# A channel norm in six parts: squares, roots and reciprocals each one part later

## The chip, the cores and the metric

The kernel runs on one core of a Trainium2 chip. The metric is the device time of one execution in microseconds. Before the change three runs took 6383.12, 6406.59 and 6412.63 us; their median is 6406.59 us. The profile is of one further execution.

The engines are named as in the profile: PE is TensorE, and PEld its weight loads; DVE is VectorE, ACT ScalarE, POOL GpSimd, and SP is the queue that issues most DMAs. "L996" is line 996 of the kernel.

## The reference, cut to what matters

Two layers run one after the other over x of shape (4, 96, 128, 128). Layer 0 is a state-space block: a projection to 192 channels, a depthwise convolution, four scans over the image in different directions, and their sum `ym`. Layer 1 is a convolution block with attention. What is touched here is the end of layer 0, a norm over the 192 channels of each pixel and the projection back to 96 channels:

```python
ym = (y0 + y1 + y2 + y3).reshape(B, D_INNER, H, W).astype(x.dtype)
yn = jnp.moveaxis(ym, 1, -1)
mu = yn.mean(-1, keepdims=True)
var = yn.var(-1, keepdims=True)
yn = (yn - mu) * jax.lax.rsqrt(var + 1e-05) * ln_w + ln_b
yn = jnp.moveaxis(yn, -1, 1)
return jnp.einsum('bdhw,cd->bchw', yn, out_w) + out_b[None, :, None, None]
...
x = x + _L0_conv_ref(_gn(x), ...)
```

The mean is taken out of the projection's weights ahead of time, so that each pixel needs only one factor, 1/sqrt(var + eps), after the projection. The variance is made as the mean of the squares minus the square of the mean.

## The kernel before, in words

The whole program is one stream of instructions for each engine, made by Python generators. A generator emits some instructions and then yields a number, the cost of what it emitted. `co_run(left, right, pace)` weaves two of them: after each yield of `left` it adds cost times pace to a debt, and as long as the debt is above zero it lets `right` emit and takes its cost off.

The four images go through the same stages. First all four are projected. The scan (`ssm_scan`) runs over pairs of images and goes on beside the rest: it works in steps of 1024 pixels for 128 channels, and each step is two halves, each with a cost of 2.6. A half-step has three operations of VectorE (`times_b` L837, `scan` L854, `times_c` L858), matmuls that spread rows into PSUM (L747), and one addition or multiplication of GpSimd. The first half also has two softplus of ScalarE (L676) and, in every other step, two exp (L809); its GpSimd operation is L833. The second half has the GpSimd addition L866, the store L875, and in every other step six loads of `xrows` on the SP queue (L735).

`ssm_output` is the norm. For image 0 it is `left` of a `co_run` with the scan at pace 0.65. For images 1 to 3 it is part of `right` (called `light`) beside the direct convolutions or the attention of the image before, at pace 1.0 or, for image 1's remainder beside the first attention, 1.5. The instructions up to the end of the scan are tied to the order of emission, engine by engine (`in_order`). After that the scheduler of the language gives each engine the instruction that is ready by its own reckoning, and among those the one emitted first.

The norm works in 16 chunks of 1024 pixels. Its loop has 18 turns. In turn c it does the first work on chunk c (`new`), the middle on chunk c-1 (`mid`), and the last on chunk c-2 (`old`). A turn has six parts, each ended by a yield:

1. the projection of `old` on PE (`projected`, L1023 and L1028), the squares and differences of `mid` (`inverse`, L996 to L998), the first squaring of `new` on ScalarE (`squares`, L959);
2. the root of `mid` on ScalarE (`roots`, L1002), the first half of `old` times its factor on VectorE (`scaled`, L1039 for image 0, L1037 for the others), the second squaring of `new`;
3. `back(mid)`: VectorE's reciprocal (L1006), GpSimd's issue of the write of `rd` (L1008), and SP's load of `xr` (L1010); then `added` for `old` on GpSimd (L1047 or L1045), the second half of `scaled`, and the first half of the means of `new` on PE (`sums`, L970);
4. the second half of `sums`, the second `added`, the statistics of the first half (`counted`, L1051), and the load of y for chunk c+1 (L951, L953);
5. `rows(new)`: ScalarE copies the means to `st` (L984 or L982) and issues four DMAs that reshape them into `mq` (L989); ScalarE adds a bias to `xr` (L1092); `spread_out(mid)` issues the read of `rd` into the tile `r` on GpSimd (L1016); the second `counted`;
6. the store of `old` (L1098).

The factor of a pixel thus passes through three DMAs: `mq` folds a row of 1024 means into 32 by 32, `rd` writes the factors to DRAM, and `r` reads them back to 96 partitions. Means of the values and of the squares lie in `mq`'s two planes.

The tiles `mq`, `xr` and `r` have two buffers each, `y` has three, `st` one. The PSUM pool of the norm has three banks in image 0 and two in the others; a chunk takes two for its projection and one for its sums.

Of the kernel before, what the change touches and what calls it, by code (L numbers as in the profile page):

```python
# [71 lines left out]
def kernel(  # L72
# [862 lines left out]
    def ssm_output(b, yms, xnew, stats, ps, side, turned):  # L935
# [5 lines left out]
        with tc.tile_pool(name="c2", bufs=2, side=side) as p2:  # L941
# [4 lines left out]
            def load_y(c):  # L946
                if c < NS:
                    y, rest = ys[c] = [
                        p2.tile([128, n], F32, name=m, bufs=3) for m, n in (("y", SN), ("yr", CH))
                    ]  # L950
                    nc.sync.dma_start(y, yms[0:128, bass.ts(c, SN)])  # L951
                    for h in range(2):
                        nc.sync.dma_start(  # L953
                            rest[64 * h : 64 * h + 64], yms[128:192, bass.ts(2 * c + h, CH)]
                        )

            def squares(c, j):
                sq = p2.tile([128, CH if j else SN], F32, name=f"sq{j}")
                nc.scalar.activation(sq, ys[c][j], AF.Square)  # L959
                sums_of[c, j] = sq  # L960

            def sums(c, j):
                sq = sums_of.pop((c, j))
                if j == 0:
                    sums_of[c] = bank(ps)
                pm = sums_of[c]
                for g in range(4):
                    rhs = sq if g % 2 else ys[c][j]
                    p = slice(64 * (g // 2), 64 * (g // 2) + 64) if j else slice(0, 128)
                    nc.tensor.matmul(  # L970
                        pm[32 * g : 32 * g + 32],
                        lhsT=mean192[p],
                        rhs=rhs[p, :] if j else rhs[:, bass.ts(g // 2, CH)],
                        start=(j == 0),
                        stop=(j == 1),
                    )
            def rows(c):
                st = p2.tile([128, CH], F32, name="st", bufs=1)
                pm = sums_of.pop(c)
                if turned:  # L980
                    to = st.rearrange("p (h j t) -> p h j t", j=TW, t=TN)
                    nc.scalar.copy(to, turned_view(pm))  # L982
                else:
                    nc.scalar.copy(st, pm)  # L984
                mq = made[c] = p2.tile([SN // TN, 2, TN], F32, name="mq")
                for i in range(2):
                    for h in range(2):
                        at = 32 * i + 64 * h
                        nc.scalar.dma_start(  # L989
                            mq[16 * h : 16 * h + 16, i],  # L990
                            st[at : at + 1].rearrange("p (a f) -> p a f", f=TN),
                        )

            def inverse(c):
                m, q = made[c][:, 0], made[c][:, 1]
                nc.vector.tensor_mul(m, m, m)  # L996
                nc.vector.tensor_sub(q, q, m)
                nc.vector.tensor_scalar(q, q, 0.0, None, ALU.max)  # L998

            def roots(c):  # L1000
                q = made[c][:, 1]
                nc.scalar.activation(q, q, AF.Sqrt, bias=eps[0 : SN // TN])  # L1002

            def back(c):
                q = made.pop(c)[:, 1]
                nc.vector.reciprocal(q, q)  # L1006
                to = rd[bass.ts(c, SN)]
                nc.gpsimd.dma_start(to.rearrange("(p f) -> p f", f=TN), q)  # L1008
                xr = p2.tile([C, SN], F32, name="xr")
                nc.sync.dma_start(xr, xb[:, bass.ts(c, SN)])  # L1010
                near[c] = xr, to

            def spread_out(c):
                xr, to = near[c]
                r = p2.tile([C, SN], F32, name="r")
                nc.gpsimd.dma_start(r, to.partition_broadcast(C))  # L1016
                near[c] = xr, r

            def projected(c):
                po = [part(ps, C, CH) for _ in range(2)]  # L1020
                y, rest = ys.pop(c)
                for h in range(2):
                    nc.tensor.matmul(  # L1023
                        po[h], lhsT=outws[:, 0], rhs=y[:, bass.ts(h, CH)], start=True, stop=False
                    )
                for h in range(2):
                    p = slice(64 * h, 64 * h + 64)
                    nc.tensor.matmul(  # L1028
                        po[h], lhsT=outws[p, 1], rhs=rest[p], start=False, stop=True
                    )  # L1030
                return po

            def scaled(c, h, po):
                r = near[c][1][:, bass.ts(h, CH)]
                if turned:
                    v = r.rearrange("p (h j t) -> p h j t", t=TN, j=TW)
                    nc.vector.tensor_mul(v, turned_view(po), v)  # L1037
                else:
                    nc.vector.tensor_mul(r, po, r)  # L1039

            def added(c, h):
                xr, r = (t[:, bass.ts(h, CH)] for t in near[c])
                if turned:
                    v = r.rearrange("p (h j t) -> p h j t", t=TN, j=TW)
                    nc.gpsimd.tensor_add(v, v, turned_view(xr))  # L1045
                else:
                    nc.gpsimd.tensor_add(xr, r, xr)  # L1047

            def counted(c, h):
                t = near[c][turned]  # L1050
                nc.vector.bn_stats(stats[:, 2 * c + h], t[:, bass.ts(h, CH)])  # L1051
# [4 lines left out]
            for c in range(NS + 2):  # L1056
                new, old = c < NS, c - 2 if c >= 2 else None
                mid = c - 1 if 1 <= c <= NS else None
                if old is not None:
                    po = projected(old)  # L1060
                if mid is not None:
                    inverse(mid)
                if new:
                    squares(c, 0)
                yield 1.2
                if mid is not None:
                    roots(mid)
                if old is not None:
                    scaled(old, 0, po[0])
                if new:  # L1070
                    squares(c, 1)
                yield 1.4
                if mid is not None:
                    back(mid)
                if old is not None:
                    added(old, 0)
                    scaled(old, 1, po[1])
                if new:
                    sums(c, 0)
                yield 1.4  # L1080
                if new:
                    sums(c, 1)
                if old is not None:
                    added(old, 1)
                    counted(old, 0)
                    load_y(c + 1)
                yield 1.4
                if new:
                    rows(c)
                if mid is not None:  # L1090
                    xr = near[mid][0]
                    nc.scalar.activation(xr, xr, AF.Identity, bias=outbs)  # L1092
                    spread_out(mid)
                if old is not None:
                    counted(old, 1)
                yield 1.4
                if old is not None:
                    nc.sync.dma_start(xnew[:, bass.ts(old, SN)], near.pop(old)[turned])  # L1098
                yield 1.4
# [1346 lines left out]
    class Image:  # L2446
# [26 lines left out]
        def norm(self, yms, ps, side):  # L2473
            yield from ssm_output(self.b, yms, self.xnew, self.stats, ps, side, self.b > 0)
# [223 lines left out]
```

## Time and profile before

| What | Value |
|---|---|
| median of three runs | 6406.59 us |
| the profiled execution's own time | 6409.68 us |
| its span, first to last instruction | 6407.8 us |
| mean granted TensorE clock | 0.902 |
| PE busy | 5253.4 us (82%) |
| DVE busy | 4699.9 us (73%) |
| ACT busy | 3759.4 us (59%) |
| POOL busy | 3238.6 us (51%) |
| norm of image 0 | 2096 to 2357 us |
| norms of images 1, 2, 3 | 3245 to 3527, 3955 to 4210, 4785 to 5035 us |

The busy shares are means over stages with different limits, so the norm has to be read from its own stretches. In a line of waits the numbers are the idle time in total, how often, and the longest. In a timeline the number in brackets is the engine's idle time before the instruction, and after the arrow stands what ended it. An instruction's duration can contain a wait inside the engine. DMA issues are not counted as busy.

### The profile page before, as it was taken

How to read it: one execution, taken by the hardware profiler on the slowest of the kernel's cores; microseconds unless marked ns; L12 is line 12 of the kernel's file. 1: busy time of each engine (PE TensorE's matmuls, PEld its weight loads, DVE VectorE, ACT ScalarE, POOL GpSimd, SP SyncE). 2: the span in 40 equal slices, each digit the busy share in tenths (PEclk: the TensorE clock that was granted, in tenths of full speed). 3: DMA queues.
4: the chain of work that ended last, by engine and by line, in shares of the span. 5: the costliest groups of instructions: out<-in, count | busy, mean ns of one | idle time of the engine just before them, and what ended most of it. 6: DMA issues, size and time to landing. Idle time of an engine off the chain costs nothing. (4 is left out here: it accounts for less than half of the span.)

```text
span 6407.8 us, 76468 instructions
## 1 busy us (share of the span) xinstructions
PE 5253.4 (82%) x23264; PEld 2254.8 (35%) x23264; DVE 4699.9 (73%) x7132; ACT 3759.4 (59%) x4770; POOL 3238.6 (51%) x2476
## 2 busy tenths in 40 slices
PE   6889988987888643989988588977888877889888
PEld 2333322322222111444433234345333444345553
DVE  4247878988989768989844686468774687988767
ACT  1247767787787666777622465466644665545642
POOL 1326757978879554979822234436304365022310
PEclk9899989998999765999999799989989888999989
DMA  6766777775675766676667686665776656967668
GB/s 155 175 160 189 198 199 199 214 221 163 198 202 171 202 183 207 196 213 179 182 185 195 166 228 163 195 169 156 214 199 184 175 149 165 245 167 180 191 168 221
DMA packets 897706, 1205.30 MB, mean 188 GB/s; under 512 B 230644, under 2 KB 745642, under 8 KB 884816
## 3 DMA queue, kind: packets, MB, share of 16 engines
q1 hardware_dynamic: 866640, 1145.36, 65.5%
q0 software_dynamic: 16336, 38.51, 2.3%
q10 hardware_dynamic: 14320, 16.54, 0.9%
q8 instruction: 187, 3.06, 0.2%
q14 instruction: 223, 1.83, 0.1%
HBM read 777.82 MB, written 345.62 MB: 175 GB/s over the span
## 5 line engine op out<-in xcount | busy, mean ns | idle before, releaser
L633 PE MATMUL bank<-y,wp 128*128 128x512 f32 (+3 forms) x3584 | 1310.9, 622 | 83.8 <-DMA y<-y 41.0
L866 POOL TENSOR_TENSOR y<-y,dl 128x1024 f32<-128x1024 f32 x384 | 1058.5, 2757 | 263.0 <-DVE dl L858 240.3
L833 POOL TENSOR_TENSOR dl<-dl,u 128x1024 f32<-128x1024 f32 x384 | 1008.8, 2627 | 253.1 <-ACT dA L809 121.1
L854 DVE TENSOR_TENSOR_SCAN dA<-dA,pBC 128x512 f32<-128x512 f32 x768 | 981.6, 1278 | 30.7
L2169 PE MATMUL bank<-y,wn 128*64 128x384 f32 (+5 forms) x2408 | 680.1, 507 | 58.3 <-DMA y<-x1d 34.1
L1477 PE MATMUL two<-ya,wd 128*64 128x192 f32 (+3 forms) x2376 | 582.2, 414 | 174.0 <-ACT odd L1550 65.1
L633 PEld LDWEIGHTS bank<-y,wp 128*128 128x128 f32 (+3 forms) x3584 | 456.2, 168 | 749.3 <-issue 651.1
L858 DVE TENSOR_TENSOR dl<-dA,pBC 128x512 f32<-128x512 f32 x768 | 528.5, 688 | 255.8 <-PE pBC L747 183.8
L747 PE MATMUL pBC<-xr,wbc 60*128 60x512 bf16 (+1 forms) x1536 | 457.8, 404 | 311.5 <-DVE dA L854 239.1
L1938 ACT COPY yb<-ya 64x768 f32<-64x768 f32 (+1 forms) x660 | 537.7, 815 | 195.5 <-PE two L1477 113.8
L676 ACT ACTIVATE dl<-pd,dtb 128x512 f32<-128x512 f32 x768 | 485.5, 684 | 187.9 <-PE pd L747 171.5
L1477 PE MATMUL two<-yb,wd 128*64 128x192 f32 (+3 forms) x2376 | 559.0, 400 | 4.0 <-ACT yb L1938 4.0
L837 DVE TENSOR_TENSOR pBC<-dl,pBC 128x512 f32<-128x512 f32 x768 | 527.5, 687 | 8.8 <-POOL dl L833 7.8
L2169 PEld LDWEIGHTS bank<-y,wn 128*64 128x64 f32 (+3 forms) x2408 | 310.3, 169 | 357.2 <-issue 186.2
L809 ACT ACTIVATE dA<-dl,negA 128x1024 f32<-128x1024 f32 x384 | 420.3, 1141 | 2.3
L1477 PEld LDWEIGHTS two<-ya,wd 128*64 128x64 f32 (+1 forms) x2376 | 262.2, 165 | 370.9 <-ACT odd L1550 75.0
L676 ACT ACT_TABLE_LOAD x248 | 318.2, 1283 | 91.9 <-PE pd L747 79.7
L747 PEld LDWEIGHTS <-wbc 60*128 60x128 bf16 (+1 forms) x1536 | 103.1, 96 | 752.1 <-issue 739.3
L1477 PEld LDWEIGHTS two<-yb,wd 128*64 128x64 f32 (+1 forms) x2376 | 289.7, 167 | 150.5 <-issue 42.1
L1477 PE MATMUL two<-ya,wa 128*96 128x384 f32 (+1 forms) x528 | 231.2, 521 | 72.9 <-DMA ya<-vp 27.0
L1550 ACT COPY odd<-two 128x384 f32<-128x384 f32 (+5 forms) x176 | 115.8, 658 | 291.3 <-PE two L1492 179.1
L1406 POOL TENSOR_TENSOR pl<-x 96x256 f32<-96x256 f32 (+3 forms) x396 | 275.2, 710 | 0.0
(322 smaller groups left out, 9105.4 us busy)
## 6 DMA issues: line engine op xcount, KB each, us to landing
u<-zb SPq DMA_DIRECT2D x192, 1024.0 KB
yms<-y SPq DMA_DIRECT2D x96, 512.0 KB
xn<-xnew SPq DMA_DIRECT2D x128, 384.0 KB
ya<-vp SPq DMA_DIRECT2D x120, 336.0 KB
y<-y SPq DMA_DIRECT2D x128, 258.2 KB
zb<-z SPq DMA_DIRECT2D x64, 512.0 KB
y<-yms SPq DMA_DIRECT2D x64, 512.0 KB
ya<-x1p SPq DMA_DIRECT2D x90, 336.0 KB
```

The lines of the kernel that those rows point to most:

```text
L633: nc.tensor.matmul(blocks(pz[p:e]), lhsT=ws[k][:, d, c : c + e - p], rhs=window(ys[k], at, d, n), start=(i == 0), stop=(i == len(terms) - 1),)
L676: nc.scalar.activation(dst, src, AF.Softplus, bias=bias)
L747: nc.tensor.matmul(p, lhsT=w[rows], rhs=xr[rows, at : at + CH], start=True, stop=True)
L809: nc.scalar.activation(live[m]["dA"], live[m]["dl"], AF.Exp, scale=negA[:, g % 3, k : k + 1])
L833: nc.gpsimd.tensor_mul(t, t, u_view(n))
L837: nc.vector.tensor_mul(p, live[n]["dl"][:, bass.ts(half, CH)], p)
L854: nc.vector.tensor_tensor_scan(h, h, p, init, ALU.mult, ALU.add)
L858: nc.vector.tensor_mul(live[n]["dl"][:, sl], live[n]["dA"][:, sl], live[n]["C", half])
L866: nc.gpsimd.tensor_add(v, v, t.rearrange("p (a b) -> p a b", b=W))
L1477: nc.tensor.matmul(of(to[p:e], r), lhsT=w[:, i, c : c + e - p], rhs=tiles(t[k][PAIR[i]][:, SLOT[i]], o, r), start=(k == 0), stop=False,)
L1938: nc.scalar.copy(yb[k][64 * h - 64 : 64 * h, :, :n], ya[k][0:64, :, h * TN : h * TN + n])
L2169: nc.tensor.matmul(pc[p:e, :n].rearrange("p (h w) -> p h w", w=W), lhsT=w[:, c : c + e - p], rhs=v[:, :, 0:W], start=(i == 0), stop=(i == ...
```

## The change

The three calls `inverse(mid)`, `roots(mid)` and `back(mid)` move from parts 1, 2 and 3 to parts 2, 3 and 4. Nothing else is changed. Inside their new part they come first, as they did in the old one: `inverse` stands ahead of `scaled(old, 0)`, `roots` ahead of `added` and `sums`, `back` ahead of the second half of `sums`. `rows`, which makes `mq`, stays in part 5, and so does `spread_out`, which reads `rd`. So there are three parts in place of two between `rows` and `inverse`, and one in place of two between `back` and `spread_out`.

```diff
@@ -1058,26 +1058,26 @@
                 mid = c - 1 if 1 <= c <= NS else None
                 if old is not None:
                     po = projected(old)
-                if mid is not None:
-                    inverse(mid)
                 if new:
                     squares(c, 0)
                 yield 1.2
                 if mid is not None:
-                    roots(mid)
+                    inverse(mid)
                 if old is not None:
                     scaled(old, 0, po[0])
                 if new:
                     squares(c, 1)
                 yield 1.4
                 if mid is not None:
-                    back(mid)
+                    roots(mid)
                 if old is not None:
                     added(old, 0)
                     scaled(old, 1, po[1])
                 if new:
                     sums(c, 0)
                 yield 1.4
+                if mid is not None:
+                    back(mid)
                 if new:
                     sums(c, 1)
                 if old is not None:
```

## The prediction

> **What bounds the kernel now.** I read the page for the span, then the busy table cut at the four norms, then the waits, over the whole run and by norm, then the timelines of single turns. Turn c is the pass of `ssm_output`'s loop with that c, in six parts; `mid` is chunk c-1, `old` is chunk c-2.
>
> The span, and the four norms (columns: stretch, its length, then busy us and instructions of PE, PEld, DVE, ACT, POOL, then granted clock, DMA share, GB/s):
>
> ```profile
> span 6407.8 us, 76468 instructions
> ...
> 2096.00:2357.00 261.00, 166.75 (x495) 34.01 (x493) 173.05 (x238) 163.97 (x187) 139.76 (x101) 0.76 0.71 208
> ...
> 3245.00:3527.00 282.00, 241.54 (x893) 88.37 (x894) 109.19 (x237) 77.83 (x124) 64.41 (x64) 0.92 0.68 186
> ...
> 3955.00:4210.00 255.00, 231.72 (x1307) 98.03 (x1307) 117.29 (x259) 119.66 (x168) 97.12 (x125) 0.98 0.65 179
> ...
> 4785.00:5035.00 250.00, 222.75 (x1239) 92.25 (x1237) 117.04 (x257) 115.16 (x162) 102.19 (x134) 0.97 0.66 186
> ```
>
> Two regimes. In image 0's norm, beside the scan, no engine passes 66%: it is a latency loop. In the other three PE is busy 86, 91 and 89%, DVE under 47%; there only PE's idle 40, 23 and 27 us can be won. The norms are 1048 of 6408 us; nothing else is touched.
>
> The waits, first of the whole run, then PE's in each of the four norms:
>
> ```profile
> POOL rd L1008 <- DVE mq L1006: 178.3, 37, 11.0
> DVE mq L996 <- DMA mq<-st: 177.3, 44, 8.6
> ...
> ACT mq L1002 <- DVE mq L998: 108.2, 39, 8.2
> ```
> ```profile
> PE bank L970 <- ACT sq L959: 54.2, 15, 7.5
> ...
> PE bank L970 <- DVE r L1037: 20.7, 6, 7.9
> ...
> PE bank L970 <- DVE r L1037: 9.8, 6, 3.7
> ...
> PE bank L970 <- DVE r L1037: 9.0, 5, 2.5
> ```
>
> VectorE, ScalarE and GpSimd stand idle on the chain that the diff moves, but PE, the bound of images 1 to 3, waits for `scaled` (L1037), which frees a PSUM bank. That stays in part 2.
>
> ScalarE in one turn of image 0 (turn 6; start, length, instruction, idle before it):
>
> ```profile
> 2176.61 2.43 ACTq L989 DMA_DIRECT2D mq<-st  x4
> 2179.09 1.15 ACT L1092 ACTIVATE xr<-xr,outbs 96x1024 f32<-96x1024 f32 x1 [2.51 <-issue]
> 2180.14 1.04 ACT L959 ACTIVATE sq<-y 128x1024 f32<-128x1024 f32 x1
> 2181.20 1.28 ACT L676 ACT_TABLE_LOAD   x1
> 2182.50 1.26 ACT L676 ACTIVATE dl<-pd,dtb 128x512 f32<-128x512 f32 x2
> 2183.78 1.28 ACT L1002 ACT_TABLE_LOAD   x1
> 2185.07 0.32 ACT L1002 ACTIVATE mq<-mq,eps 32x32 f32<-32x32 f32 x1
> 2185.30 0.61 ACT L959 ACTIVATE sq<-yr 128x512 f32<-128x512 f32 x1
> 2187.95 0.58 ACT L984 COPY st<-bank 128x512 f32<-128x512 f32 x1 [2.03 <-PE bank L970]
> ```
>
> With the four issues counted, ScalarE is full except for 2.03 us between `sq<-yr` and the copy, in which PE makes the sums of that square. The root and its table load sit in front of that square.
>
> VectorE in turns 6 and 13, the parts that matter:
>
> ```profile
> 2179.99 0.18 DVE L996 TENSOR_TENSOR mq<-mq 32x32 f32<-32x32 f32 x1
> 2180.47 2.60 DVE L997 TENSOR_TENSOR mq<-mq 32x32 f32<-32x32 f32 x1 [0.30 <-DMA mq<-st]
> ...
> 2293.33 0.34 DVE L1006 RECIPROCAL mq<-mq 32x32 f32<-32x32 f32 x1 [5.52 <-ACT mq L1002]
> ```
>
> A 32x32 subtraction that takes 0.18 us elsewhere takes 2.60 while GpSimd multiplies (L833, 2180.64 to 2183.02), and a reciprocal holds VectorE for 5.52 us until the root is done.
>
> **What the Trainium skill says.** "SBUF — State Buffer", Who interferes with whom: a VectorE instruction with two SBUF inputs and a GpSimd instruction that reads SBUF exclude each other, and the later one blocks fully. The 0.18 against 2.60 us agrees. "ScalarE: Activation LUTs", What ACT_TABLE_LOAD costs: 1283 ns for every change of set; the trace has a mean of 1283 ns. "DMA: Bandwidth & Descriptors", Anatomy of one DMA: about 2 us fixed, mostly the receipt of the last write. The trace is longer, 4.2 us median to landing for `mq<-st` and 4.4 for `rd<-mq`, and those durations are used.
>
> **The change part by part.** Nothing is added or removed. Per chunk three small VectorE operations (0.18+0.18+0.17 us), one root (0.32, with a 1.28 us load), one reciprocal (0.34), the GpSimd issue of `rd` (0.54) and SP's load of `xr` move. What counts is what they are moved past.
>
> *Image 0* is held to the order of emission. The norm's parts cost 1.2 and 1.4, times the pace 0.65: 0.78 and 0.91; a half-step of the scan costs 2.6. So two half-steps fall in a turn (A with softplus, B without): after parts 2 and 5 in turns 1 to 4, after 1 and 4 in turns 5 to 10, after 6 and 3 in turns 11 to 16. The engines' order in the trace agrees. Only in turns 5 to 10 do the squares cross any scan work; elsewhere they stay between the same VectorE instructions.
>
> Turns 5 to 10 (turn 6 by hand). A starts at 2180.0 and not 2183.2, ends 2182.8; the squares follow, free of the GpSimd multiply at 2183.0, done 2183.7. On ScalarE `sq<-yr` comes at 2183.8 and not 2185.3, and the root (1.28+0.32) falls into the 2.03 us in which the copy waits. ScalarE's loop shrinks by 1.6. But `scaled` cannot start before r lands, and that loop grows: `scaled` to reciprocal now has both halves ahead of it (0.69+0.66=1.35 for 0.65), then 0.7 to the issue of rd, 6.4 to its landing (mean of these six), 0.4, 4.9 for r: 13.9 us, where it was 13.2. The pitch was 14.7 (2166.1 to 2239.8, five turns), so 0.8 a turn is left: 6 x 0.8 = -5 us. GpSimd then stands some 1.3 us longer before the r issue, since only one addition and L866 lie between; what is queued behind it is L833 of the next step, which VectorE needs a half-step later: hidden.
>
> Turns 11 to 16 (turns 12 and 13). The reciprocal moves behind B (2.75 us), the rd issue behind L866 (2.35): in turn 12 rd goes at 2280.5 for 2277.2, r lands 3 us later (2290 for 2287.0). In turn 13 the reciprocal no longer blocks B, which starts at 2291.3 for 2294.1; r lands 2 us earlier there (2301.4 for 2303.4). Over a pair that is no loss, and ScalarE's 1.6 can come through: the copy waited 1.2 to 3.6 us here too. On SP the `xr` load falls behind six `xrows` loads (5.46 us) in three turns; ScalarE's L1092 waits for it, I take 1 us each. 6 x -1.6 + 3 = -7 us.
>
> Turns 1 to 4. The root moves behind softplus and exp of A. In turn 1 that makes rd 4.5 us later and r's landing 2.8 after the old start of `scaled`; after that 0.7 a turn (the second half of `scaled` ahead of the reciprocal), partly returned because `sq<-yr` no longer waits for the squares (3.9 us in turn 3). +4 us.
>
> Image 0: -5 -7 +4 = -8 us.
>
> *Images 1 to 3* are ordered by the scheduler, near the order of emission. Counting there in the kernel before, other VectorE work lies between parts 1 and 2 in only 9 of 48 turns; in the other 39 the squares wait at the same place, and the 162 us of waits in these three windows stay. ScalarE gets one to three attention operations and `sq<-yr` ahead of the root in most turns: its waits for the squares (49.9+24.1+30.1) shrink, but ScalarE is busy under half of the time and PE waits little for it. Against this the rd issue may fall behind `added` (1.53 us), in the dozen of 45 turns where only its rank put it in front. r arrives last before `scaled` in 21 of 48 turns, so a dozen times 1.5 us half passed on is some +5; the 9 crossings and freed ScalarE some -5. I take 0; the bounds are -22 and +24 (rivals).
>
> Sum: -8 us. Against the profiled execution (6409.7 us, 1.9 outside its span) 6401.7; against the median of the runs, 6406.6, it is 6399.
>
> **Rivals.** *Faster.* ScalarE's loop sets image 0 alone: 12 turns x -1.6 = -19, the roots' waits in turns 2 to 4 another -5; and in images 1 to 3 half of PE's 45 us of waits for `scaled` (39.5 above and 5.8 at L1023 in image 1) go, -22. 6360 us. For it: 21 `scaled` start right behind squares that waited for mq. Against it: the squares still stand ahead of `scaled`, and r's landing follows `scaled` with 0.1 to 1.9 us of slack.
>
> *Slower.* One mechanism: r lands later, because reciprocal and rd go one part later while the r issue stays. It decides where the slip passes r's slack, 0.9 us on the mean for the chunks of turns 5 to 10. Image 0: turn 12's 3 us in all six late turns and not in every other, +18, and +4 early; images 1 to 3: 21 turns with r last x 1.5 us, three quarters reaching PE, +24. 6452 us. For it: L1016 already waits 46.2 us for rd in 18 turns, with two parts of room. Against it: in 22 of 45 turns the scheduler put the reciprocal ahead of `scaled` by readiness, where rank doesn't matter.
>
> *It does nothing* in three quarters of the turns, and the order elsewhere settles to the same pitch: 6407.
>
> **How the numbers follow.** No two runs tell a difference under about 0.5% (32 us). Likeliest with its near neighbour "nothing": 0.46, own range 6378 to 6432, almost all inside 0.5%. Faster rival 0.28, slower 0.26, each mostly beyond 0.5%. Hence 0.28, 0.46, 0.26. The range reaches to both rivals, with 1 in 10 outside on each side: 6348 to 6456.
>
> **What would show it.** Right: in image 0 the copy L984's wait for PE falls from 25.4 us to a few, the reciprocal's 21.9 us wait for the root goes, L1016's wait for rd and L1039's for r (7.8) grow; image 0's norm ends some 8 us earlier. In images 1 to 3 the wait L996 for mq stays near 160 us and PE's idle time within 10 us. Wrong, if L996's wait falls by half and PE's waits for L1037 with it (faster), or L1037's wait for r rises beyond 80 us (slower), or if the scheduler lays images 1 to 3 out anew.

## The result, and the profile after

The changed kernel takes 6419.09 us in the median of 22 runs (6403.12 to 6436.19), the kernel before 6405.17 in 22 runs beside them (6383.12 to 6414.72). The ratio is 1.0023, with a 95% interval of 1.0014 to 1.0032: 15 us slower, 9 to 20. When it was run again later beside others the ratio was 1.0017 (1.0007 to 1.0026). The forecast was 6399, so a small gain was expected and a small loss came; it lies inside the range, and inside the half per cent that the prediction called no change.

The span and the four norms of the kernel after (columns as before: stretch, length, busy us and instructions of PE, PEld, DVE, ACT, POOL, granted clock, DMA share, GB/s):

```profile
span 6415.1 us, 76484 instructions
...
2100.00:2359.00 259.00, 161.26 (x496) 33.01 (x493) 170.18 (x237) 163.47 (x187) 139.74 (x100) 0.76 0.73 209
3236.00:3534.00 298.00, 251.19 (x917) 91.80 (x915) 117.46 (x250) 79.69 (x128) 66.66 (x64) 0.91 0.65 181
3942.00:4205.00 263.00, 238.37 (x1340) 102.97 (x1340) 118.99 (x262) 125.26 (x175) 103.12 (x135) 0.98 0.65 183
4775.00:5039.00 264.00, 236.29 (x1252) 95.53 (x1248) 119.34 (x263) 116.34 (x164) 102.19 (x135) 0.95 0.63 179
```

Here each stretch runs from the first load of y to the last statistics of the image. With these borders the four norms of the profiled kernel before took 260.3, 289.6, 263.5 and 250.8 us; those of the kernel after 258.9, 298.1, 263.0 and 263.6. In image 3's norm PE does the same 1252 matmuls, but is busy for 236 us, where the kernel before needed 227 in the same borders, at a clock of 0.95 where it had 0.97. The kernel before, there:

```profile
4781.00:5032.00 251.00, 226.62 (x1252) 94.34 (x1248) 117.89 (x263) 116.82 (x164) 102.20 (x135) 0.97 0.67 189
```

The waits of the whole run that the prediction had shown, in the kernel after:

```profile
DVE mq L996 <- DMA mq<-st: 179.6, 44, 8.3
...
POOL rd L1008 <- DVE mq L1006: 137.1, 37, 9.7
ACT mq L1002 <- DVE mq L998: 135.3, 40, 9.2
```

VectorE's wait for the folded means (177.3 before) has hardly moved. PE's largest wait by total in each of the four norms, in order:

```profile
PE bank L970 <- ACT sq L959: 39.1, 13, 7.2
...
PE bank L970 <- DVE r L1037: 23.7, 5, 9.7
...
PE two L1477 <- ACT odd L1550: 7.6, 3, 3.4
...
PE bank L970 <- DVE r L1037: 12.2, 5, 4.5
```

In image 0, PE waits less for the square: 39.1 us for 54.2. In images 1 and 3 it waits 3 us more for `scaled`, in image 2 3 us less (6.8 for 9.8).

ScalarE in turn 6 of image 0, kernel after:

```profile
2183.44 1.15 ACT L1092 ACTIVATE xr<-xr,outbs 96x1024 f32<-96x1024 f32 x1 [2.57 <-DMA mq<-st]
2184.49 1.04 ACT L959 ACTIVATE sq<-y 128x1024 f32<-128x1024 f32 x1
2185.55 1.28 ACT L676 ACT_TABLE_LOAD   x1
2186.85 1.26 ACT L676 ACTIVATE dl<-pd,dtb 128x512 f32<-128x512 f32 x2
2188.00 0.63 ACT L959 ACTIVATE sq<-yr 128x512 f32<-128x512 f32 x1
2188.65 1.28 ACT L1002 ACT_TABLE_LOAD   x1
2189.94 0.32 ACT L1002 ACTIVATE mq<-mq,eps 32x32 f32<-32x32 f32 x1
2190.17 0.56 ACT L984 COPY st<-bank 128x512 f32<-128x512 f32 x1
```

This is what the prediction drew by hand: the square `sq<-yr` now stands ahead of the root and its table load, and the copy L984 follows the root without a wait (2.03 us before). What took its place stands in VectorE's waits in image 0's norm:

```profile
DVE r L1039 <- DMA r<-rd: 25.0, 13, 3.9
DVE xstats L1051 <- POOL xr L1047: 14.6, 11, 1.6
DVE mq L1006 <- ACT mq L1002: 13.7, 4, 5.7
```

`scaled` (L1039) now waits for r, the factors on their way back to 96 partitions, 13 times and 25.0 us, where it waited 4 times and 7.8 us; the reciprocal's wait for the root fell from 21.9 to 13.7.

### The profile page after: what moved, and what is told of

It is laid out like the page before. It is cut to its first block, busy times and chain, and to the rows that moved or that the text cites. A ratio compares the mean times of both kernels' runs of the same rounds, so it can differ in the third digit from the quotient of the medians.

```text
span 6415.1 us, 76484 instructions
## 1 busy us (share of the span) xinstructions
PE 5258.1 (82%) x23264; PEld 2259.2 (35%) x23264; DVE 4702.3 (73%) x7132; ACT 3759.1 (59%) x4770; POOL 3241.7 (51%) x2476
## 5 line engine op out<-in xcount | busy, mean ns | idle before, releaser
L866 POOL TENSOR_TENSOR y<-y,dl 128x1024 f32<-128x1024 f32 x384 | 1059.3, 2759 | 268.6 <-DVE dl L858 248.9
L833 POOL TENSOR_TENSOR dl<-dl,u 128x1024 f32<-128x1024 f32 x384 | 1009.9, 2630 | 247.2 <-ACT dA L809 127.7
L1477 PE MATMUL two<-ya,wd 128*64 128x192 f32 (+3 forms) x2376 | 583.7, 416 | 177.1 <-ACT odd L1550 71.7
L858 DVE TENSOR_TENSOR dl<-dA,pBC 128x512 f32<-128x512 f32 x768 | 528.8, 689 | 263.3 <-PE pBC L747 191.4
L2169 PE MATMUL bank<-y,wn 128*128 128x384 f32 (+5 forms) x2408 | 672.2, 505 | 54.9 <-DMA y<-x1d 29.7
L1477 PE MATMUL two<-yb,wd 128*64 128x192 f32 (+3 forms) x2376 | 563.1, 401 | 3.9 <-ACT yb L1938 3.9
L2169 PEld LDWEIGHTS bank<-y,wn 128*128 128x128 f32 (+3 forms) x2408 | 308.5, 168 | 347.6 <-issue 172.1
L1477 PEld LDWEIGHTS two<-ya,wd 128*64 128x64 f32 (+1 forms) x2376 | 262.6, 166 | 372.0 <-ACT odd L1550 82.7
L676 ACT ACT_TABLE_LOAD x248 | 318.2, 1283 | 100.1 <-PE pd L747 87.4
L1477 PEld LDWEIGHTS two<-yb,wd 128*64 128x64 f32 (+1 forms) x2376 | 291.0, 167 | 156.3 <-issue 48.2
L1477 PE MATMUL two<-ya,wa 128*96 128x384 f32 (+1 forms) x528 | 231.2, 522 | 72.1 <-DMA ya<-vp 29.8
```

Of the source, the lines that this page charges most:

```text
L676: nc.scalar.activation(dst, src, AF.Softplus, bias=bias)
L833: nc.gpsimd.tensor_mul(t, t, u_view(n))
L858: nc.vector.tensor_mul(live[n]["dl"][:, sl], live[n]["dA"][:, sl], live[n]["C", half])
L866: nc.gpsimd.tensor_add(v, v, t.rearrange("p (a b) -> p a b", b=W))
L1477: nc.tensor.matmul(of(to[p:e], r), lhsT=w[:, i, c : c + e - p], rhs=tiles(t[k][PAIR[i]][:, SLOT[i]], o, r), start=(k == 0), stop=False,)
L2169: nc.tensor.matmul(pc[p:e, :n].rearrange("p (h w) -> p h w", w=W), lhsT=w[:, c : c + e - p], rhs=v[:, :, 0:W], start=(i == 0), stop=(i == ...
```

## The experiments

The whole effect is 0.2%, and the 22 executions of the kernel before spread over 0.5%. So each run below was timed against the kernel before, with an interval, and its profiled execution was also cut into stages. The length of a norm repeats better than the whole: image 0's norm took 257.0 to 260.6 us in the seven profiled runs with the old parts there, and image 3's 247.7 to 255.4 us in the eight in which the load of `xr` there kept its place.

Three theories stood at the start. *A*: the loss is made in images 1 to 3, where the step moved last (reciprocal, `rd`, load of `xr`) lays the work out anew, and image 0 gives nothing, since r takes over from ScalarE as the last to arrive. *B*: the loss is made in image 0, by r's later landing (the prediction's slower rival). *C*: it is only a redistribution that any small shift makes.

### One part of the images, one part of the moves

Image 0 alone. In the code `turned` is false for image 0 and true for the others; each move is made under a condition:

```diff
-                if mid is not None:
-                    inverse(mid)
+                if mid is not None and turned: inverse(mid)
...
+                if mid is not None and not turned: inverse(mid)
+                if mid is not None and turned: roots(mid)
...
+                if mid is not None and not turned: roots(mid)
+                if mid is not None and turned: back(mid)
...
+                if mid is not None and not turned: back(mid)
```

> All three moves in image 0 alone; images 1 to 3 as in the kernel before. Theory A (the loss is made in images 1 to 3, where the later reciprocal, rd issue and xr load lay the work out anew; image 0 gives nothing since the arrival of r takes over from ScalarE as the last wait before scaled): the time of before within 6 us, image 0's norm within 4 us of its old 260, scaled gated by r in some 13 of 16 turns as in the kernel after. Theory B (the loss is made in image 0, by r's later landing): 8 to 16 us slower, and the norms of images 1 and 3 as before. Theory C (what the profile of after shows in images 1 and 3 is a redistribution that any small shift upstream makes): images 1 and 3 move here by several us too, though their order of work is that of before.

Images 1 to 3 alone: the same edit with the two conditions exchanged.

> All three moves in images 1 to 3 alone; image 0 as before. Theory A: 12 to 22 us slower than before, of which norm 1 some 8 to 10, norm 2 about 0, norm 3 some 11 to 13, as in the profile of after. Theory B: within 5 us of before. Theory C: somewhere between, with norms 1 and 3 not repeating their 9 and 12 us.

The last step alone, in all images:

```diff
-                if mid is not None:
-                    back(mid)
                 if old is not None:
                     added(old, 0)
...
                 yield 1.4
+                if mid is not None:
+                    back(mid)
                 if new:
                     sums(c, 1)
```

> Only the reciprocal, the rd issue and the xr load one part later, in all four images; squares and roots stay. Theory A: images 1 to 3 lose as in the kernel after (12 to 22 us), because this step alone changes their order; and in image 0 r lands later with nothing won on ScalarE, some 6 to 15 us more: 18 to 35 us slower than before. Theory B: as slow as after or somewhat more (14 to 30 us), all of it in image 0. Theory C: images 1 to 3 not worse than before by more than 5 us.

No part moved, but the root last in its part:

```diff
-                if mid is not None:
-                    roots(mid)
                 if old is not None:
                     scaled(old, 0, po[0])
                 if new:
                     squares(c, 1)
+                if mid is not None:
+                    roots(mid)
                 yield 1.4
```

> Nothing moved between parts; in part 2 the first half of scaled and the second square are emitted ahead of the root, so in image 0 the square no longer stands behind the root and its table load, and the reciprocal and the rd issue keep their place. The order of images 1 to 3 is that of before. If ScalarE's root ahead of the square set image 0's pitch and r's landing follows only 0.1 to 1.9 us behind: 4 to 12 us faster than before, the copy L984's wait for PE under 18 us (25.4 before). If r's landing takes over at once, as in the kernel after: within 4 us of before, with more than 10 of 16 scaled gated by r.

Measured (time against the kernel before with its 95% interval; then the four norms of the profiled execution in us):

| run | time | norm 0 | norm 1 | norm 2 | norm 3 |
|---|---|---|---|---|---|
| before | | 260.3 | 289.6 | 263.5 | 250.8 |
| after | +0.23% (0.14 to 0.32) | 258.9 | 298.1 | 263.0 | 263.6 |
| image 0 alone | +0.17% (0.08 to 0.26) | 262.3 | 295.5 | 265.5 | 254.9 |
| images 1 to 3 alone | +0.11% (0.01 to 0.21) | 257.1 | 291.4 | 267.5 | 265.6 |
| last step alone | +0.16% (0.07 to 0.26) | 266.0 | 291.8 | 268.0 | 263.3 |
| root last in its part | +0.06% (-0.04 to 0.16) | 254.3 | 295.4 | 260.4 | 248.9 |

The profile of after had shown norm 1 and norm 3 longer, and both had been taken for effects. Norm 1 was chance: in the runs with its old order it took 295.5 and 295.4, and with the new one 291.4 and 291.8. Norm 3 stands: near 264 in all three runs with the last step moved there, at or below 255 in the others. In image 0 the last step alone costs 7 us of norm, the root behind the square gains 4. With the root last, L984's wait for PE fell from 25.4 to 10.4 us as expected of a gain, but 10 of the 16 `scaled` then waited for r, and the whole time did not fall. C holds for norm 1 and falls for norm 3, which repeats. In time A missed: images 1 to 3 alone were 7 us slower (1 to 14), where it had 12 to 22, and the last step alone 10 (4 to 17), where it had 18 to 35. And the time of the run with image 0 alone, +11 us (5 to 17), is more than its norm shows and not the "within 6" of A, so B was not out yet.

### Which part of the last step

Two theories for the loss in images 1 to 3 are told apart here. *X*: the place of the load of `xr` in the order of emission makes the scheduler lay out the engines anew. *R*: the later reciprocal and `rd` make r late. `back` was split into its two halves, so that they could stand in different parts:

```diff
-            def back(c):
-                q = made.pop(c)[:, 1]
-                nc.vector.reciprocal(q, q)
+            def back(c, rd_part=True, xr_part=True):
+                q = made.pop(c)[:, 1] if rd_part else None
+                if rd_part: nc.vector.reciprocal(q, q)
                 to = rd[bass.ts(c, SN)]
...
+                if rd_part: nc.gpsimd.dma_start(to.rearrange("(p f) -> p f", f=TN), q)
+                xr = p2.tile([C, SN], F32, name="xr") if xr_part else None
+                if xr_part: nc.sync.dma_start(xr, xb[:, bass.ts(c, SN)])
+                if xr_part: near[c] = xr, to
```

In images 1 to 3, only the load of `xr` later (part 3 calls `back(mid, True, not turned)`, part 4 `back(mid, False, True)` where turned):

> Images 1 to 3: only the load of xr one part later; reciprocal and rd issue stay. Image 0 as before. Theory X (the place of the xr load in the order of emission is what makes the scheduler lay out the engines anew, and norm 3 loses by it): norm 3 takes 264 us (251.5 is the mean of the three runs with the order of before), with over 25 us of half clock in it (17 to 20 before), PE waits some 4 to 5 us for the attention's sm 54 us after its start; norms 1 and 2 within 4 us; the time 8 to 16 us up. Theory R (the later reciprocal and rd make r late, as the slower rival of the prediction had it): norm 3 stays at 249 to 255 us, the time within 5 us of before.

In images 1 to 3, only the reciprocal and the `rd` issue later:

> Images 1 to 3: only the reciprocal and the rd issue one part later; the load of xr stays. Image 0 as before. Theory X: norm 3 stays at 249 to 255 us with 17 to 21 us of half clock; the time within 5 us of before. Theory R: norm 3 at 260 us or more, scaled gated by r oftener than 7 times in it, the time 8 to 16 us up.

The whole change in all images, except that the load of `xr` stays in part 3:

> The whole change in all images except that the load of xr stays in its old part. The order of work on SP and PE is then that of the kernel before, but for two places. Theory X (the later load of xr relays PE's order in images 1 to 3, which splits pairs of matmuls and makes long gaps with half clock after them): norm 3 at 249 to 256 us (263.8 is the mean of four runs with all of the last step moved), norm 2 at 261 to 266, full-speed PE work in norm 3 at 217 to 220 us and not 223; the time 10 to 15 us below the changed kernel's and within 6 us of before. Theory R (the later reciprocal and rd issue cost it): norm 3 above 259 us, the time 8 to 18 us above before.

The load of `xr` in images 1 to 3 one part earlier, nothing else moved:

> Only the load of xr in images 1 to 3, one part earlier than in the kernel before, nothing else moved. If any other place of the load relays the order and costs (the old order is a good one by luck): 5 to 15 us slower, norms 2 and 3 above 268 and 256 us. If it is lateness that costs: within 5 us of before or faster, norms 2 and 3 at or below 264 and 252.

| run | time | norm 0 | norm 1 | norm 2 | norm 3 |
|---|---|---|---|---|---|
| load of xr later | +0.02% (-0.08 to 0.11) | 260.1 | 290.9 | 269.8 | 255.4 |
| reciprocal and rd later | -0.03% (-0.12 to 0.06) | 260.6 | 292.7 | 264.3 | 251.9 |
| all but the load of xr | +0.08% (-0.01 to 0.16) | 260.8 | 294.0 | 265.3 | 247.7 |
| load of xr earlier | +0.28% (0.19 to 0.37) | 257.1 | 292.1 | 271.2 | 256.6 |

Theory R (r late) falls for images 1 to 3: with reciprocal and `rd` later, but the load in place, norm 3 is as it was, and in the whole change without the load it is the shortest of all. Theory X holds for the structure, not for its size: the load alone makes PE's new order, but norm 3 then takes 255.4 us, not 264, and the time is that of before. In these profiles, one of each kernel, only both halves together give the 264. Nor does the time of the run with all but the load follow its norm: it is 5 us above before (-1 to 10) and only some 6 below the changed kernel that was timed beside it, where 10 to 15 were forecast; more on this below. The earlier load is the slowest of these runs, so it is not lateness alone that costs. It gave PE another order in norms 1 and 2; in norm 3 the order stayed that of the kernel before, and the norm took 256.6 us all the same.

What the new order is can be read on PE, 50 us into image 3's norm. The kernel before:

```profile
4827.83 0.90 PE L1770 MATMUL two<-ident,ring 96*90 96x96 f32 x8 [1.97 <-ACT odd L1550]
4830.05 1.71 PE L970 MATMUL bank<-y,mean 128*32 128x512 f32 x2 [1.32 <-DVE r L1037]
4831.69 2.02 PE L1023 MATMUL bank<-y,outws 128*96 128x512 f32 x2
...
4852.85 1.10 PE L1028 MATMUL bank<-yr,outws 64*96 64x512 f32 x4
```

The kernel after at the same place:

```profile
4824.00 0.90 PE L1770 MATMUL two<-ident,ring 96*90 96x96 f32 x8 [0.23 <-ACT odd L1550]
4828.79 1.65 PE L1477 MATMUL two<-ya,wd 128*128 128x384 f32 x2 [3.89 <-DVE sm L1656]
4830.37 1.06 PE L970 MATMUL bank<-y,mean 128*32 128x512 f32 x1
...
4852.90 1.10 PE L1028 MATMUL bank<-yr,outws 64*96 64x512 f32 x2
4853.93 1.10 PE L1023 MATMUL bank<-y,outws 128*96 128x512 f32 x2
4854.95 1.10 PE L1028 MATMUL bank<-yr,outws 64*96 64x512 f32 x2
```

After L1770 the attention must wait for VectorE's `sm`. Before, the norm's sums and projection (L970, L1023) stood in that gap. Now two attention matmuls (L1477) stand first, and PE waits 3.89 us in one piece. In the other four runs with the whole last step in image 3 this wait is 4.3 to 5.3 us. The stretches around it in the kernel after (the gap, the 10 us behind it, the 11 us after those):

```profile
4825.00:4829.00 4.00, 0.21 (x1) 0.21 (x2) 2.37 (x5) 3.13 (x4) 1.55 (x2) 0.81 0.98 316
4829.00:4839.00 10.00, 10.00 (x23) 1.63 (x24) 3.35 (x9) 1.02 (x2) 1.97 (x2) 0.56 0.20 55
4839.00:4850.00 11.00, 11.00 (x35) 4.30 (x36) 2.86 (x7) 4.39 (x7) 8.45 (x13) 1.00 0.65 180
```

Behind the gap PE is busy without a pause, but for 10 us at a clock of 0.56: an L970 takes 1.06 us, where it takes 0.59 to 0.63 at full clock. So the wait of 4 us costs another 4 to 5 us that no line of waits shows. The kernel before stood nearly as long at this place, but in two pieces (1.97 and 1.32 us), and ran 3.4 us at half clock behind them; the kernel after ran 10.2.

The second loss is in the last lines of the two fences, which show the same chunk, the fifth. The projection of a chunk ends with two pairs of L1028, one for each half of the partitions. All four together take as long as two, 1.03 us to the start of what follows. Where another matmul stands between the pairs, each pair takes its own 1.03. In image 3's norm 12 chunks have all four together and 4 are split in every run with the old order; with the later load 9 and 7. Three chunks more make 3.1 us. In norms 1 and 2 the later load splits no chunk more: 10 and 8 of 16 are split in the kernel before and in the kernel after. This goes with their not getting longer.

### Which image

All moves in image 3 alone (`b == 3` in place of `turned`, `b != 3` for the old places):

> All moves in image 3 alone. If the loss of images 1 to 3 lies in norm 3: the norm takes 264 us with over 25 us of half clock, the other three as in the kernel before, and the time is 10 to 14 us up. If what norm 3 shows depends on how images 1 and 2 ended, and not on its own order: 249 to 255 us, the time within 5 us.

All moves in images 0, 1 and 2, and in images 1 and 2 alone:

> All moves in images 0, 1 and 2; image 3 as before. If the lengths of the norms tell the split (norm 3 +12, image 0 +2, norms 1 and 2 about 0): norm 3 at 248 to 255 us, full-speed PE work in it at 217 to 220 us, and the time only 0 to 5 us above before. If the timed split of the single-image runs is the right one (image 0 some 11, images 1 to 3 some 7): 10 to 16 us above.

> All moves in images 1 and 2 alone. By the lengths of the norms: within 4 us of before, so that the run with image 0 moved too lies 0 to 4 us above this one. By the timed split: the run with image 0 moved too lies 8 to 14 us above this one.

The changed kernel again:

> The changed kernel once more, beside the two above on the same chip: 12 to 18 us slower than before, norm 3 at 261 to 267 us with over 25 us of half clock.

| run | time | norm 0 | norm 1 | norm 2 | norm 3 |
|---|---|---|---|---|---|
| image 3 alone | +0.07% (-0.01 to 0.16) | 257.0 | 299.4 | 263.4 | 262.6 |
| images 0, 1, 2 | +0.02% (-0.10 to 0.15) | 261.3 | 292.8 | 266.3 | 251.8 |
| images 1, 2 | -0.01% (-0.12 to 0.10) | 257.1 | 291.7 | 267.7 | 255.4 |
| after, again | +0.17% (0.07 to 0.26) | 261.7 | 288.9 | 263.6 | 261.3 |

Taken out of image 3 alone, the change costs nothing that can be measured, +1 us (-6 to 10), which speaks for the norms' split. Put into image 3 alone, it made the norm longer as forecast, but the time came out 4 us up (-1 to 10) where 10 to 14 were forecast, and the changed kernel's own 11 (4 to 17) lies just under its 12 to 18. So the norm's length repeats, while the times are too coarse to confirm all of it. The stretch behind norm 3 gives nothing clear back: it took 1373 us on the mean of the five runs with the whole step moved in image 3, and 1375 in the eight with the load in place. Image 3's norm, one line each, in the run with images 1 to 3 alone, with image 3 alone, with the change in the other three images, and with all but the load:

```profile
4773.00:5039.00 266.00, 241.94 (x1254) 97.03 (x1252) 118.53 (x263) 116.48 (x164) 102.18 (x135) 0.93 0.64 178
```
```profile
4772.00:5035.00 263.00, 235.61 (x1251) 97.05 (x1250) 117.87 (x263) 116.11 (x164) 102.32 (x135) 0.95 0.64 180
```
```profile
4776.00:5028.00 252.00, 226.71 (x1252) 94.47 (x1250) 117.01 (x262) 116.68 (x165) 102.36 (x135) 0.97 0.67 188
```
```profile
4790.00:5038.00 248.00, 223.32 (x1252) 93.59 (x1250) 117.40 (x263) 116.46 (x164) 102.27 (x135) 0.98 0.68 190
```

The same 1252 matmuls, within 2, cost 223 to 227 us of PE where the load is in its old place, and 236 to 242 where the whole step is moved (over all runs 223 to 231, and 236 to 242). Over all runs, with the time under half clock taken from the trace's record of the granted clock, and the busy time counted down by half of its share under half clock ("full speed"):

| image 3's norm, means | norm | PE idle | PE busy | of it at full speed | half clock |
|---|---|---|---|---|---|
| load of xr in its old place there, 8 runs | 252.1 | 25.2 | 226.9 | 218.0 | 18.2 |
| whole last step moved there, 5 runs | 263.3 | 26.2 | 237.1 | 223.3 | 30.7 |
| load of xr alone, 1 run | 255.4 | 27.6 | 227.8 | 224.1 | 10.2 |

The 11.2 us are 1.0 of idle time, 5.3 of more work at full speed (3.1 of them the split L1028), and 10.2 - 5.3 = 4.9 of half clock. The load alone brings the work but not the half clock. In that run the wait for `sm` was 4.2 us long too, and it drew only 6.8 us of half clock. So it did with all moves in image 3 alone: in these two half clock ended 4.0 and 4.1 us behind the wait, in the four other runs 8.7 to 9.5 us behind it. The recorded clock changes in steps of 3.41 us. In the two runs the first whole step behind the wait began with the attention's L1477 (29 and 30% of it), and the next was at full clock; in the four L1477 fell into the step in which the wait ended, the first whole step was L970 for 80 to 100%, and one more at half clock followed. So in these six runs the half clock that a wait of 4 to 5 us draws goes with where it falls on the steps. In the rest of the norm the run with the load alone had 3.4 us of half clock, the five others 17 to 27; why is open, and it is one profile.

Left open as well: the run with image 0 alone was 5 to 17 us slower, though by the two runs above image 0's share is 2 us (+0.02% against -0.01%, a difference known to some 10 us), and by its norm 2.6. And in the run with all but the load, and in both with the load alone moved, the stretch between norms 2 and 3 took 581 to 584 us, where it took 565 to 576 in the twelve others without the later r of the next section. In the run with all but the load PE does the same 2301 matmuls there in the very order of the kernel before, with no more idle time and no more work at full speed, but with 184 us of half clock where that kernel had 143; with the earlier load it is 184 too. The three profiled executions were also 4 to 14 us above the medians of their kernels. So this is likelier scatter of single executions; an effect of the load on that stretch is not shown.

### Image 0: is r the floor?

Squares and roots later in image 0, the last step in place (the conditional edit of the first experiment without its `back`):

> Image 0: squares and roots one part later, reciprocal, rd issue and xr load in their old part; images 1 to 3 as before. If the gain that the prediction put on ScalarE (the square no longer behind the root) is real and the later reciprocal and rd issue give it back: image 0's norm takes 252 to 256 us (258.7 is the mean of two runs with the old order, 260.6 of two with all moves, 266.0 with only the last move), and the time is 3 to 7 us down. If the later squares and roots gain nothing: 258 to 261 us.

Measured: -0.03% (-0.13 to 0.08), norm 0 257.3 us, a gain of 1.2 against the seven old runs and less than the 252 to 256 forecast. VectorE now waited 12 times and 33.2 us for r. That suggested theory *F*: r's landing is the floor of image 0's turn. Its rival *G*: other work of the turn, in its fixed order, sets the pitch. For a test, in image 0 the chunk that is projected and scaled became c-3, so that r has a turn more; y has four buffers then, r three and `sq0` one, and the load of `xr` and its bias go with chunk c-2.

```diff
-            for c in range(3):
-                load_y(c)
+            lag = 2 if turned else 3
+            for c in range(lag + 1): load_y(c)
...
-            for c in range(NS + 2):
-                new, old = c < NS, c - 2 if c >= 2 else None
-                mid = c - 1 if 1 <= c <= NS else None
+            for c in range(NS + lag):
+                new, old = c < NS, c - lag if c >= lag else None
+                mid, far = (c - n if n <= c < NS + n else None for n in (1, lag - 1))
...
+                if far is not None: load_x(far)
```

> Order of the parts as in the kernel before, but in image 0 the chunk that is projected and scaled is c-3 and not c-2 (four y buffers, three r, one sq0, the load of xr and its bias a turn later), so r has a turn more to land. Theory F (r's landing is the floor of image 0's turn): scaled gated by r in at most 2 of 16 turns (6 to 8 before), image 0's norm 245 to 255 us in spite of the one turn more at its end (259 before). Theory G (other work of the turn, ScalarE's, VectorE's and the scan's in their fixed order, sets the pitch, and r only happens to arrive last): also hardly gated by r, but the norm 257 to 265 us. The extra turn shifts the order of images 1 to 3 too, so the whole time is no test of either.

> As the run with r a turn later in image 0, and there with all of the change's moves too. Theory F: now that r has room, the moves give what the prediction put on ScalarE: image 0's norm 6 to 12 us shorter than in the run with the old parts. Theory G: within 3 us of it.

> As the run with r a turn later in image 0, with the second square ahead of the root there and nothing else moved. Theory F: image 0's norm 6 to 12 us shorter than with the root first (without the later r, it was 254.3 against 259). Theory G: within 3 us of it.

> r a turn later in all four images (one buffer for each of the two squares), the parts as in the kernel before. Images 1 to 3: if PE's waits for scaled (40 us in the three norms, with the half clock that follows them) come from r's landing, these waits fall below 15 us and norms 1 to 3 together (805 us before) lose 20 to 40 us, the whole time 15 to 45 us down. If they come from VectorE's order or the squares' wait for mq ahead of scaled, the waits stay above 25 us and the norms within 10 us.

Image 0's norm, cut at the starts of L996 in turns 1, 5, 11 and 16, in us (what is left is start and tail):

| image 0's order | norm 0 | turns 1-4 | turns 5-10 | turns 11-15 |
|---|---|---|---|---|
| old, 7 runs | 258.5 | 57.2 | 87.9 | 78.6 |
| all moves, 4 runs | 261.1 | 59.7 | 85.0 | 80.5 |
| last step alone | 266.0 | 58.6 | 87.8 | 84.9 |
| squares and roots alone | 257.3 | 61.7 | 87.6 | 74.3 |
| root last in its part | 254.3 | 55.0 | 90.3 | 74.2 |
| r a turn later | 269.9 | 61.8 | 85.6 | 80.9 |
| r a turn later, all moves | 264.5 | 54.8 | 84.9 | 82.3 |
| r a turn later, root last | 266.4 | 61.4 | 87.8 | 76.1 |

With r a turn later VectorE did not wait for it once in image 0, and turns 5 to 15 took 166.5 us, as they had (87.9 + 78.6). So theory F falls: r's landing was not the floor of the old loop. The single buffer of `sq0` doesn't hide a gain, since no square of that run waited for PE. The moves on top changed these turns by 0.7 us; what they gained, 5.4 us of norm 0, between the two forecasts, lies in turns 1 to 4. So it is not r alone that holds back their gain. The norm itself came out above both forecasts, 269.9 us: 4.6 more in turns 1 to 4 and 6.0 more at its tail, where the one turn more is. With the root last it was 3.5 shorter, between the two. What VectorE and GpSimd wait for then, in the run with r a turn later:

```profile
DVE mq L1006 <- ACT mq L1002: 27.0, 8, 7.1
DVE xstats L1051 <- POOL xr L1047: 26.3, 17, 1.8
DVE mq L996 <- DMA mq<-st: 21.9, 5, 7.4
```
```profile
POOL rd L1008 <- DVE mq L1006: 63.6, 11, 12.0
POOL r L1016 <- DMA rd<-mq: 20.1, 7, 6.6
```

The other waits of the chain are all still there. GpSimd stands 63.6 us for the reciprocal and 20.1 for `rd`, with the scan's L833 and L866 behind it in its queue. Which of these loops is the tightest was not settled. The whole time of these runs (+0.62%, +0.49%, +0.66%) is no measure, since the one turn more shifts the order of images 1 to 3.

With r a turn later in all images: +0.61% (0.48 to 0.73). There PE's waits for `scaled` in norms 1 to 3 fell from 45.3 us to 5.2, as expected, and the norms did not shrink with them: 302.5, 266.3 and 249.6, together 818 for 804. The order of all work was another, so this doesn't say what the waits are worth; it says that they can be had without any gain. No version that was run beats the kernel before beyond its interval.

## Why the prediction was wrong

Two terms of the sum failed, by about as much each: images 1 to 3 and image 0.

*Images 1 to 3, taken as 0.* The step that failed is that the moved load of `xr` was put at nothing there. The term measured 11 us of norm length, all in image 3 (norms 1 and 2 changed by -1.9 and +2.1 us on the mean). The prediction counted what lies between the parts on VectorE and ScalarE and where `rd` might fall; that part was right (VectorE's wait for `mq`, 161.8 us in the prediction's three windows, became 168.1, "near 160"; the run with reciprocal and `rd` alone changed nothing). It costed SP's load of `xr` in image 0 only. In images 1 to 3 the same load went unpriced, and it is the one move there that lays PE's work out anew. The prediction named "if the scheduler lays images 1 to 3 out anew" among the things that would make it wrong, without a price or a place.

*PE's idle time as the only thing to win or lose.* The test "PE's idle time within 10 us" came true (91 us in the three norms by the prediction's lines, 99 by those of the kernel after; norm 3 in its borders: 24.4 to 27.7) and was blind: the loss is in PE's busy time. The page "TensorE: Matmul & The Clock Gate" of the Trainium skill, in "What's actually happening", says that the clock is halved after a window of some 3.4 us without work; the trace agrees in the length of the step, 3.41 us, and the last section says where it goes further. The clock column stood beside the quoted lines (0.97 in norm 3), and the prediction didn't read it as a price of waits. Nor did it read that pairs of L1028 overlap only side by side.

*Image 0, -8.* It measured +2.6, four runs against seven. By the prediction's own stretches: turns 1 to 4, +4 forecast, +2.5 measured; turns 5 to 10, -5 and -2.9; turns 11 to 16, -7 and +1.9 (to the start of turn 16's L996), with 1.1 more at start and tail. So the step that failed in image 0 is that of the last six turns. Both halves of it were seen: squares and roots alone do gain there, 4.3 us (ScalarE's 1.6 a turn would have been 8.0 in these five), but the last step alone costs 6.3, where the prediction let the early and late landings of r in turns 12 and 13 cancel. The sum of the two, +2.0, is what all moves give. GpSimd's queue shows it, first in the kernel before, then in the run with the last step alone:

```profile
POOL r L1016 <- DMA rd<-mq: 21.4, 9, 5.4
```
```profile
POOL r L1016 <- DMA rd<-mq: 38.8, 12, 5.2
```

With one part of room and not two, the issue of r waits for `rd` in 12 turns where it waited in 9. The -5 of turns 5 to 10 also has a slip of addition: its terms for r's loop make 13.75 us and not 13.9, which would have given -6.

*The named tests.* L984's wait for PE fell from 25.4 to 15.5, not to a few. The reciprocal's wait for the root fell from 21.9 to 13.7 and did not go. L1016's wait for `rd` grew from 21.4 to 24.0 and L1039's for r from 7.8 to 25.0, as named.

*Two readings.* The 1283 ns that the prediction gives as the price of a change of set are the table load alone; the page that it names adds a drain and puts the whole at 2.66 us. In ScalarE's lines the load starts 0.02 us after the instruction before it has ended, and the next follows as closely, so the 1.28 us used is what this trace shows. Of VectorE and GpSimd, which exclude each other there, the subtraction that stood had the earlier start (2180.47 us, GpSimd's 2180.64): the lines show the exclusion, but not that the later one blocks.

*The rivals.* The slower one had the sign, not the mechanism: in images 1 to 3, L1037's wait for r went from 40.6 to 49.6 us, far from the 80 that would have decided, and the run with the later reciprocal alone lost nothing. In image 0 its mechanism is there (6.3 us in turns 11 to 15), a third of the 18 it gave. The faster one's condition, PE's waits for `scaled` halved, did not occur.

## What to carry to other kernels

Where a scheduler orders the work, a move of the least important instruction, here a load that PE doesn't wait for, can change the order of the engine that bounds; price every moved instruction there, and test with one move at a time. Read a busy engine's time together with its clock and its count: the same 1252 matmuls took 227 and 237 us. Where a small effect hides in the scatter of the whole, cut the profiled executions into stages and compare the stage over all runs; a single profile showed norm 1 longer by 8 us, and that was nothing.

## What the runs showed of the hardware

The granted clock of PE is recorded in steps of 3.41 us, each full or half. In norms 1 to 3 of fifteen profiled runs (all but those with r a turn later), a step that followed one in which PE was busy for under 40% ran at half clock in 199 of 199 cases, after 40 to 50% in 58 of 86, after 80% and more in 53 of 2837. All of these 53 followed a step that itself ran at half clock; after a full-clock step with PE busy for 60% and more, half clock followed in 2 of 2825 cases. The way back asks for more: after a half-clock step with PE busy for under 80%, the next one was at half clock in 111 of 111 cases. So a wait need not fill a step: after pauses of 3.5 us and more half clock followed within 12 us in every case, with a mean of 5 to 6 us of it after 3.5 to 4.5 us, and 11 after 5 and more (counted from the pause's start, other pauses nearby included); after pauses of 0.3 to 1 us, in about a quarter of the cases. The Trainium skill's page gives the window and the halving; that a window with up to 40% of work draws it too is from these traces.
